# Cross-attention on one core: x in four buffers instead of one, and the last store in two halves

## The chip, the cores and the metric

The kernel runs on one core of a Trainium2 chip. The metric is the device time of one execution in microseconds (us). The core has five engines that run side by side and meet only at semaphores: TensorE (PE) multiplies matrices, VectorE (DVE) and ScalarE (ACT) work element by element, GpSimd (POOL) reduces over partitions and issues the DMAs that add to what lies at their destination, and SyncE (SP) issues most other DMAs. Each engine works through its own instructions in order; so does each engine's list of DMAs to issue: a DMA whose wait has not ended holds up those behind it.

## What is computed

For each of 8 batches, with x1 = x and x2 = the context, both 512 channels by 1024 positions, 32-bit floats:

```python
q = jnp.einsum('bcn,dc->bnd', x1, Wq) + bq
k = jnp.einsum('bcn,dc->bdn', x2, Wk) + bk[:, None]
v = jnp.einsum('bcn,dc->bdn', x2, Wv) + bv[:, None]
attn = jax.nn.softmax(jnp.einsum('bnd,bdm->bnm', q, k), axis=2)
attn_out = jnp.einsum('bcm,bnm->bcn', v, attn)
return attn_out + x1
```

q and k have 64 channels, v and the result 512.

## The kernel before

The batches run one after the other, but overlap: `period` works on the second half of batch `s` (products of the exponentials with the context, then with the value weights) and, between them, on the scores and exponentials of the next batch `n`, the query projection of the one after it, `nn`, and a load for `nnn`. The order of all instructions on every engine is the order in which the code issues them (`tc.manual_schedule()`); the tile framework adds only the semaphore waits.

The large products are not done plainly: they are split into 2 by 2 blocks and computed with seven block products (the names "11" to "22", "S1" to "S4", "T1" to "T4" and the numbers 1 to 7 are those of Strassen's scheme in Winograd's form), many of them split once more in the same way. The sums of blocks that this needs are made on DVE (`left_stream`, `right_stream`, lines 521 to 543), on ACT with a sign, or by accumulating DMAs that POOL issues: `add_t4` (line 360) adds T2 into T4, which ACT filled with the negative of another block; `right_stream(s, 4, ...)` reads T4 on DVE (line 536, name `eI4eT`). The softmax's denominators go over a small chain: POOL reduces (line 290), a DMA reorders one row (292), DVE takes the reciprocal (298), two DMAs spread it (300, 306), and DVE scales with it (874).

**x.** x is read in a form of 128 partitions by 4 tiles (of 128 channels) by 1024 positions. One buffer with the tag "x" holds it, and it is used by turns: `load_x` (line 133) takes the buffer for x1 of a batch, the query projection reads it, `load_x` takes it again for x2 of the same batch, the key projection reads it, and so on. The four tiles are loaded by four DMAs of 512 KB on SP's queue (line 137). Since a buffer is given anew only when all that touched it has ended, the first of the four waits for all matmuls of the projection before; the other three follow it without such a wait.

**Projections.** `project` (line 182; also `keys_parts`, line 405, for batch 1) does eight products, four tiles by two halves of the positions, tile by tile, and accumulates in one bank. The trace counts 16 matmul records for them (L190 or L413). `next_queries` (line 1127) projects the queries and then loads x2; `next_keys` (line 1134) projects the keys and then loads x1 of the batch after.

**Head.** Batch 0 has its own start (`head`, line 1010). x1 comes in the buffer "x", first its left half in four DMAs (line 1031), then its right half in two DMAs of two tiles each (line 1037); x2 comes in another buffer, in eight DMAs between them (line 1034). Behind these in SP's queue stand four tiles `a` of the context in another layout (line 144) and four tiles of the value weights `w` (line 97). DVE sums two of the `a` tiles at line 109 and then subtracts the maximum from the scores (line 315); ACT takes their exponentials, and the first product (line 463) uses them.

**Tail.** In the last batch x1 stays in the buffer "x", and the result is added into it. POOL adds one block (`tmp[6]`) into two tiles with one DMA (line 1454); DVE adds the others (lines 621, 905, 923, 952, 955) and SP stores each piece as it is ready (lines 924, 953). `finish` (line 957) adds the last two pieces (line 961) and stores them (line 962): 256 KB, then 128 KB of 128 partitions by 256 positions.

SP's DMAs of the whole kernel signal on eight semaphores in turn, and a DMA waits until the one before it on the same semaphore, eight places back, has landed.

Of the kernel before, what the change touches and what calls it, by code (L numbers as in the profile page):

```python
# [15 lines left out]
def kernel(  # L16
# [115 lines left out]

    def load_x(s, x):

        s.x = sb.tile([P, CT, N], F32, tag="x", name=f"x_{s.b}_{x.tensor.name}")
        for c in range(CT):
            nc.sync.dma_start(s.x[:, c, :], x[s.b, ts(c, P), :])

    def load_a(s, *ks):
        for k in ks:  # L140
# [41 lines left out]
    def project(s, nm, w_sb, bank=None):  # L182

        if bank:
            ps = ps_a.tile([P, H], F32, tag=bank, name=f"ps_{nm}_{s.b}")
        else:
            ps = ps_s.tile([P, H], F32, tag="s", name=f"ps_{nm}_{s.b}")
        for c in range(CT):
            for h, r in ((0, lo), (1, hi)):
                nc.tensor.matmul(  # L190
                    ps[r, :],
                    w_sb[:, c, :],
                    s.x[:, c, ts(h, H)],
                    start=(c == 0),
                    stop=(c == CT - 1),
                )
        return ps
# [207 lines left out]
    def keys_parts(s):  # L405

        ps = ps_s.tile([P, H], F32, tag="s", name=f"ps_k_{s.b}")
        s.k = sb.tile([P, H], F32, tag="k", name=f"k_{s.b}")

        def add(*tiles):  # L410
            for c in tiles:
                for h, r in ((0, lo), (1, hi)):
                    nc.tensor.matmul(  # L413
                        ps[r, :], wk_sb[:, c, :], s.x[:, c, ts(h, H)], start=(c == 0), stop=(c == CT - 1)
                    )
            if c == CT - 1:
                nc.scalar.activation(s.k, ps, AF.Identity, bias=bk_sb)

        return add
# [169 lines left out]
    def multiply_573(s):  # L589

        s.inner["o7"], s.inner["o3"] = inner_w["o7"], inner_w["o3"]
        a = [ps_a.tile([P, H], F32, tag=f"a{j}", name=f"ps_oa{j}_{s.b}_7") for j in range(2)]
        chain, third = inner_parts(s, "o7")
        d = [ps_s.tile([P, H], F32, tag="s", name=f"ps_od{j}_{s.b}_3") for j in range(2)]
        for j in range(2):
            s.bank["a", j], s.bank["d", j] = a[j], d[j]
        v = sb.tile([P, H], F32, tag="top", name=f"vo73_{s.b}", bufs=2)
        v7, v3, copy = v[:, left], v[:, right], nc.scalar.copy
        u5 = s.tmp[5] = sb.tile([P, 2, H], F32, tag="u5", name=f"uo5_{s.b}")
        a0, a1, d0, d1 = ([x[:, left], x[:, right]] for x in (*a, *d))  # L600
# [16 lines left out]

        def add_v(k, v):
            r, h = int(k[0]) - 1, int(k[1]) - 1
            x = s.x[:, 2 * r + 1, ts(h, H)].rearrange("p (a n) -> p a n", a=2)  # L620
            nc.vector.tensor_tensor(x, x, v.unsqueeze(1).to_broadcast([P, 2, H // 2]), ALU.add)

        for x in ORDER573:
            if x[0] == 5:
                j, k = divmod(x[1], 2)
                ps = s.bank["c", j]
                nc.tensor.matmul(
                    ps,
                    w["S1"][:, k, ts(j, P)],
                    s.y["T1"][:, k, :],  # L630
                    start=False,
                    stop=k == 1,
                    skip_group_check=True,
                )
                if k == 1:
                    copy(u5[:, j, :], ps)
                    for q in ("22", "12"):
                        with_x1(s, q, j)
            elif x[0] == 4:
                part, k = divmod(x[1], 2)  # L640
                if x[1] == 2:
                    s.bank["last"] = last = ps_a.tile([P, H], F32, tag="c0", name="ps_last")
                if x[1] == 0:
                    last_left(s, True)
                    evict_o(s, "12", rows=(0,))
                ps, j, n = ((a[0], 0, slice(0, H)), (last, 1, left), (a[1], 1, right))[part]
                nc.tensor.matmul(
                    ps[:, n],
                    w["22"][:, k, ts(j, P)],
                    s.y["T4"][:, k, n],  # L650
                    start=part == 1 and k == 0,
                    stop=k == 1,
                    skip_group_check=True,
                )
            else:
                i, z = f"o{x[0]}", x[1]
                ps, opens, copies = steps[x]
                inner_product(s, i, z, ps, opens)
# [242 lines left out]
    def with_x1(s, k, j):  # L901

        r, h = int(k[0]) - 1, int(k[1]) - 1
        x = s.x[:, 2 * r + j, ts(h, H)]
        nc.vector.tensor_tensor(x, x, s.tmp[6 if k == "21" else 5][:, j, :], ALU.add)

    def evict_o(s, k, hook=None, rows=range(2)):
# [11 lines left out]

        if s.b == B - 1:  # L920
            for j in rows:
                o = s.x[:, 2 * r + j, ts(h, H)]
# [24 lines left out]

    def last_left(s, second=False):

        o = s.x[:, 3, left]  # L950
        if second:
            nc.vector.tensor_tensor(o, o, s.bank["last"][:, left], ALU.add)
            nc.sync.dma_start(out[s.b, ts(3, P), left], o)
        else:
            nc.vector.scalar_tensor_tensor(o, s.bank["a", 1][:, left], bv_sb[3], o, ALU.add, ALU.add)

    def finish(s):

        for j, n in ((0, slice(0, H)), (1, right)):
            o = s.x[:, 2 + j, n]  # L960
            nc.vector.scalar_tensor_tensor(o, s.bank["a", j][:, n], bv_sb[2 + j], o, ALU.add, ALU.add)
            nc.sync.dma_start(out[s.b, ts(2 + j, P), n], o)

    def add_tile(s, h, i):
        nc.gpsimd.dma_start(s.mx[h], s.e[h][:, :, i, :], accum_op=ALU.add)  # L965
# [11 lines left out]
    def head_queries(s, x_sb, h, n, bank=None):  # L977
# [6 lines left out]
        def add(*tiles):  # L984
            for c in tiles:
                for r in (lo, hi):
                    nc.tensor.matmul(
                        ps[r, n], wq_sb[:, c, :], x_sb[:, c, ts(h, H)][:, n], start=(c == 0), stop=(c == CT - 1)
                    )
            if c == CT - 1:  # L990
                nc.scalar.activation(s.q[:, ts(h, H)][:, n], ps[:, n], AF.Identity, bias=bq_sb)
# [18 lines left out]
    def head(s):  # L1010
# [5 lines left out]

        s.q = sb.tile([P, N], F32, tag="q", name=f"q_{s.b}", bufs=2)
        s.k = sb.tile([P, H], F32, tag="k", name=f"k_{s.b}")
        x1_sb = sb.tile([P, CT, N], F32, tag="x", name="x1_head")
        x2_sb = sb.tile([P, 2, MH, H], F32, tag="e1", name="x2_head")  # L1020
        s.x = x2_sb.rearrange("p t c (h n) -> p c t h n", h=2)

# [17 lines left out]
        load_a(s, "21", "22", "11", "12")  # L1040
        load_values()
        tiles = range(CT)
# [70 lines left out]
    def period(s, n, nn, nnn):  # L1113
# [337 lines left out]
        if n:  # L1451
            add_x1(s, "21")
        else:
            nc.gpsimd.dma_start(s.x[:, 2:4, 0:H], s.tmp[6], accum_op=ALU.add)
        if s.b == 0:
            negate(n, "S3")
            add_11(n, "S3")
# [111 lines left out]
```

## Time and profile before

| | |
|---|---|
| time, three runs | 665.46, 665.56, 666.08 us (median 665.56) |
| the profiled execution: its time | 666.55 us |
| its span, from the first to the last instruction | 664.7 us |
| PE busy | 659.7 us (99%) |
| DVE busy | 615.8 us (93%) |
| ACT busy | 378.6 us (57%) |
| POOL busy | 224.2 us (34%) |
| granted TensorE clock | 1.0 throughout |
| moved by DMA | 135.88 MB, mean 204 GB/s |

Times in the profile's views are from the start of the span. A "line" such as L137 is the line of the kernel before that issued the instruction; of a helper that is called from several places there is one line. "PE" is a matmul, "PEld" its weight load, "SPq" the queue of SP. A row of the timeline gives start, duration, engine, line, operation, what it writes and reads, how many instructions are merged, and in brackets how long the engine was idle before and what ended that. A row of a line's own view gives the shortest, median and longest duration in nanoseconds and the first and last start; the row "DMA to landing" gives the shortest, median and longest time from the issue of a DMA to its completion.

### The profile page before, as it was taken

The numbers are of one execution on the slowest core, as the hardware profiler recorded it, in microseconds if no ns is written. First come the engines' busy times: TensorE is split into PE (matmuls) and PEld (weight loads), VectorE is DVE, ScalarE is ACT, GpSimd is POOL, SyncE is SP. The second block draws the span as 40 slices with busy tenths as digits, with TensorE's granted clock in tenths as the row PEclk, the third lists the DMA queues.
The fourth block names the chain that finished last, engine by engine and source line by source line (L and its number), as shares of the span: only waits on it lengthen the run. The fifth ranks groups of instructions, "written<-read, shape, count | busy, mean of one in ns | idle before, by whom it ended". The sixth has DMA issues, their size and how long they took to land.

```text
span 664.7 us, 7983 instructions
## 1 busy us (share of the span) xinstructions
PE 659.7 (99%) x2626; PEld 433.7 (65%) x2626; DVE 615.8 (93%) x865; ACT 378.6 (57%) x723; POOL 224.2 (34%) x192
## 2 busy tenths in 40 slices
PE   9999999999999999999999999999999999999997
PEld 5435754757658666686666776666865757666865
DVE  0989999999999989999899989999899999999997
ACT  2855467345574674755756647656467455584332
POOL 0125215531245402553124631254214640244300
PEclk9999999999999999999999999999999999999999
DMA  8688576996799869999599995899946996399504
GB/s 326 260 239 270 142 231 143 188 237 215 233 184 224 237 183 284 160 227 243 168 280 185 253 226 163 259 200 235 267 98 169 207 255 194 73 181 240 128 22 150
DMA packets 51545, 135.88 MB, mean 204 GB/s; under 512 B 5680, under 2 KB 6192, under 8 KB 51504
## 3 DMA queue, kind: packets, MB, share of 16 engines
q0 software_dynamic: 24512, 61.94, 50.1%
q1 hardware_dynamic: 26704, 73.15, 30.7%
q8 instruction: 21, 0.34, 0.2%
q10 hardware_dynamic: 288, 0.28, 0.2%
q14 instruction: 20, 0.16, 0.1%
HBM read 87.83 MB, written 16.81 MB: 157 GB/s over the span
## 4 chain that ended last, share of the span: by engine, by line
PE 96%; DMA 3%; SPq 0%; DVE 0%; issue 0%
PE ps_yc L554 9%; PE ps_oc L463 8%; PE ps_ya L554 7%; PE ps_s L235 6%; PE ps_oa L688 6%; PE ps_oa L463 5%; PE ps_ya L463 4%; PE ps_q L190 4%; PE ps_i5chain L554 3%; PE ps_i4b L839 3%; PE ps_k L190 3%; PE ps_i3chain L554 3%; PE ps_i7chain L554 3%; PE ps_oc L839 3%; PE ps_i2chain L554 3%; PE ps_i1chain L554 3%
## 5 line engine op out<-in xcount | busy, mean ns | idle before, releaser
L330 ACT ACTIVATE e<-e 128x1024 f32<-128x1024 f32 x60 | 63.4, 1059 | 29.3 <-DVE e L321 28.3
L321 DVE TENSOR_TENSOR e<-e,top 128x1024 f32<-128x1024 f32 x60 | 72.7, 1219 | 2.1 <-POOL top L271 2.1
L290 POOL PARTITION_ALL_REDUCE den<-sum x16 | 52.8, 3299 | 63.7 <-DVE sum L265 58.8
L271 POOL PARTITION_ALL_REDUCE top<-max x16 | 29.9, 1868 | 98.3 <-DVE max L265 50.0
L965 POOL DMA_DIRECT2D sum<-e x21 | 25.6, 1219 | 103.0 <-ACT sum L970 39.4
L244 ACT COPY e<-ps_s 128x512 f32<-128x512 f32 x90 | 47.8, 620 | 10.1 <-PE ps_s L235 7.6
L235 PE MATMUL ps_s<-q,k 64*128 64x512 f32 (+1 forms) x188 | 46.9, 599 | 0.0
L255 DVE TENSOR_TENSOR max<-max,e 128x1024 f32<-128x1024 f32 x30 | 36.6, 1220 | 0.3
L235 PEld LDWEIGHTS ps_s<-q,k 64*128 64x128 f32 x188 | 17.4, 186 | 19.9 <-issue 17.3
L874 DVE TENSOR_TENSOR y<-y,den 128x1024 f32<-128x1024 f32 x24 | 29.2, 1222 | 0.3
L463 PE MATMUL ps_oa<-yT,w_S 128*128 128x512 f32 x64 | 28.8, 593 | 0.0
L463 PE MATMUL ps_oc<-yT,w 128*128 128x512 f32 x64 | 28.8, 592 | 0.0
L745 ACT COPY ps_yc<-ps_i7chain 128x256 f32<-128x256 f32 x32 | 11.4, 357 | 30.2 <-PE ps_i7chain L554 24.7
L306 POOL DMA_DIRECT2D den<-row x12 | 6.7, 560 | 59.7 <-DMA row<-few 39.0
L521 DVE TENSOR_TENSOR aI<-a,aI 128x256 f32<-128x256 f32 x60 | 25.3, 422 | 0.6
L521 DVE TENSOR_TENSOR aI<-a 128x256 f32<-128x256 f32 x60 | 25.8, 451 | 0.0
L190 PE MATMUL ps_q<-x_in_x_dram,wqk_sb 128*64 128x512 f32 x112 | 25.6, 598 | 0.0
L745 ACT COPY ps_ya<-ps_i5chain 128x256 f32<-128x256 f32 x32 | 11.5, 360 | 24.1 <-PE ps_i5chain L554 20.0
L745 ACT COPY ps_ya<-ps_i1chain 128x256 f32<-128x256 f32 x28 | 10.0, 357 | 24.7 <-PE ps_i1chain L554 21.1
L554 PE MATMUL ps_yc<-e,aI 128*128 128x256 f32 x92 | 23.6, 379 | 0.0
L688 PE MATMUL ps_oa<-yT,w_S 128*128 128x512 f32 x48 | 23.5, 592 | 0.0
L941 POOL DMA_DIRECT2D r<-in_x_dram x14 | 23.3, 1662 | 0.0
(348 smaller groups left out, 1840.0 us busy)
## 6 DMA issues: line engine op xcount, KB each, us to landing
x_in_x_dram<-in_x_dram SPq DMA_DIRECT2D x60, 512.0 KB, 8.2
a<-in_x2T_dram SPq DMA_DIRECT2D x32, 512.0 KB, 7.1
aS<-in_x2T_dram POOLq DMA_DIRECT2D x21, 512.0 KB, 11.0
sum<-e POOLq DMA_DIRECT2D x21, 512.0 KB, 5.4
eT<-eT POOLq DMA_DIRECT2D x16, 512.0 KB, 11.7
uo<-in_x_dram POOLq DMA_DIRECT2D x14, 512.0 KB, 10.4
r<-in_x_dram POOLq DMA_DIRECT2D x14, 512.0 KB, 8.8
out_dram<-r SPq DMA_DIRECT2D x14, 512.0 KB, 8.4
```

What stands on the lines that cost most here:

```text
L190: nc.tensor.matmul(ps[r, :], w_sb[:, c, :], s.x[:, c, ts(h, H)], start=(c == 0), stop=(c == CT - 1),)
L235: nc.tensor.matmul(ps[g][:, n], s.k[r, ts(i, P)], s.q[r, ts(h, H)][:, n], start=True, stop=True)
L244: nc.scalar.copy(e[:, g, i, :], ps[g])
L255: nc.vector.tensor_tensor(f, e[:, :, 0, :] if i == 1 else f, e[:, :, i, :], op)
L290: nc.gpsimd.partition_all_reduce(s.den[h], s.mx[h][:, 0, :], P, ReduceOp.add)
L321: nc.vector.tensor_tensor(e, e, top, ALU.subtract)
L330: nc.scalar.activation(e, e, AF.Exp)
L463: nc.tensor.matmul(ps, left[ka][:, k, ts(j, P)], right[kb][:, k, :], start=opens and k == 0, stop=i in (2, 3, 4) and k == n_k - 1, skip_gr ...
L521: nc.vector.tensor_tensor(v[k], v[x], v[y], op)
L554: nc.tensor.matmul(ps, s.inner[i][ka][:, k, :], s.inner[i, "t"][kb][:, k, :], start=opens and k == 0, stop=z in (2, 3, 4) and k == n_k - 1 ...
L688: nc.tensor.matmul(ps, w[ka][:, k, ts(j, P)], s.y[kb][:, k, :], start=False, stop=i == 3 and k == 1, skip_group_check=True,)
L839: nc.tensor.matmul(ps, s.inner[i][ka][:, k, :], s.inner[i, "t"][kb][:, k, :], start=opens and k == 0, stop=z in (2, 3, 4) and k == n_k - 1 ...
```

## The change

The buffer of 4 tiles becomes four buffers "x0" to "x3", each of which is given anew when all that read that tile has ended. So each load waits for the matmuls of its own tile. `s.x` becomes a list, and what indexes it follows. The transfers that went over two tiles are split: in the head the two DMAs of the right half of x1 become four, one per tile, and in the tail POOL's one DMA into two tiles becomes two. Besides, the very last store becomes two, partitions 0 to 63 on SP's queue and 64 to 127 on ACT's.

```diff
     def load_x(s, x):
 
-        s.x = sb.tile([P, CT, N], F32, tag="x", name=f"x_{s.b}_{x.tensor.name}")
+        s.x = []
         for c in range(CT):
-            nc.sync.dma_start(s.x[:, c, :], x[s.b, ts(c, P), :])
+            s.x.append(sb.tile([P, N], F32, tag=f"x{c}", name=f"x{c}_{s.b}_{x.tensor.name}"))
+            nc.sync.dma_start(s.x[c], x[s.b, ts(c, P), :])
...
-                    s.x[:, c, ts(h, H)],
+                    s.x[c][:, ts(h, H)],
...
     def finish(s):
 
         for j, n in ((0, slice(0, H)), (1, right)):
-            o = s.x[:, 2 + j, n]
+            o = s.x[2 + j][:, n]
             nc.vector.scalar_tensor_tensor(o, s.bank["a", j][:, n], bv_sb[2 + j], o, ALU.add, ALU.add)
-            nc.sync.dma_start(out[s.b, ts(2 + j, P), n], o)
+            if j:
+                for queue, r in ((nc.sync, lo), (nc.scalar, hi)):
+                    queue.dma_start(out[s.b, ts(2 + j, P), n][r], o[r])
+            else:
+                nc.sync.dma_start(out[s.b, ts(2 + j, P), n], o)
...
-        x1_sb = sb.tile([P, CT, N], F32, tag="x", name="x1_head")
+        x1_sb = [sb.tile([P, N], F32, tag=f"x{c}", name=f"x{c}_head") for c in range(CT)]
...
         for c in range(CT):
-            nc.sync.dma_start(x1_sb[:, c, 0:H], x1[s.b, ts(c, P), 0:H])
+            nc.sync.dma_start(x1_sb[c][:, 0:H], x1[s.b, ts(c, P), 0:H])
...
-        for c in (0, 2):
-            nc.sync.dma_start(
-                x1_sb[:, c : c + 2, H:N], x1[s.b, c * P : (c + 2) * P, H:N].rearrange("(t p) n -> p t n", p=P)
-            )
+        for c in range(CT):
+            nc.sync.dma_start(x1_sb[c][:, H:N], x1[s.b, ts(c, P), H:N])
...
-            nc.gpsimd.dma_start(s.x[:, 2:4, 0:H], s.tmp[6], accum_op=ALU.add)
+            for j in range(2):
+                nc.gpsimd.dma_start(s.x[2 + j][:, 0:H], s.tmp[6][:, j, :], accum_op=ALU.add)
```

More of the change, by code (lines that the diff above doesn't have):

```diff
@@ L413, in add @@
                     nc.tensor.matmul(
-                        ps[r, :], wk_sb[:, c, :], s.x[:, c, ts(h, H)], start=(c == 0), stop=(c == CT - 1)
+                        ps[r, :], wk_sb[:, c, :], s.x[c][:, ts(h, H)], start=(c == 0), stop=(c == CT - 1)
                     )
@@ L619, in add_v @@
             r, h = int(k[0]) - 1, int(k[1]) - 1
-            x = s.x[:, 2 * r + 1, ts(h, H)].rearrange("p (a n) -> p a n", a=2)
+            x = s.x[2 * r + 1][:, ts(h, H)].rearrange("p (a n) -> p a n", a=2)
             nc.vector.tensor_tensor(x, x, v.unsqueeze(1).to_broadcast([P, 2, H // 2]), ALU.add)
@@ L903, in with_x1 @@
         r, h = int(k[0]) - 1, int(k[1]) - 1
-        x = s.x[:, 2 * r + j, ts(h, H)]
+        x = s.x[2 * r + j][:, ts(h, H)]
         nc.vector.tensor_tensor(x, x, s.tmp[6 if k == "21" else 5][:, j, :], ALU.add)
@@ L921, in evict_o @@
             for j in rows:
-                o = s.x[:, 2 * r + j, ts(h, H)]
+                o = s.x[2 * r + j][:, ts(h, H)]
                 nc.vector.scalar_tensor_tensor(o, s.bank[bank, j], bias(j), o, ALU.add, ALU.add)
@@ L948, in last_left @@
     def last_left(s, second=False):
-        o = s.x[:, 3, left]
+        o = s.x[3][:, left]
         if second:
@@ L987, in add @@
                     nc.tensor.matmul(
-                        ps[r, n], wq_sb[:, c, :], x_sb[:, c, ts(h, H)][:, n], start=(c == 0), stop=(c == CT - 1)
+                        ps[r, n], wq_sb[:, c, :], x_sb[c][:, ts(h, H)][:, n], start=(c == 0), stop=(c == CT - 1)
                     )
```

## The prediction

> **What bounds the kernel now.** I read the page's busy times and chain first, then busy time by stretch, then the stretches where TensorE (PE) is not full.
>
> ```profile
> span 664.7 us, 7983 instructions
> ...
> PE 659.7 (99%) x2626; PEld 433.7 (65%) x2626; DVE 615.8 (93%) x865; ACT 378.6 (57%) x723; POOL 224.2 (34%) x192
> ...
> PE 96%; DMA 3%; SPq 0%; DVE 0%; issue 0%
> ```
>
> PE is busy for 659.7 of 664.7 us, and the chain that ends last is 96% PE. All that waits less can give back is the 5.0 us in which PE stands idle, if "busy" is honest; busy time by stretch says where those 5.0 us lie and lets "busy" be tested.
>
> ```profile
> 0.00:25.43 25.43, 24.05 (x140) 13.20 (x140) 9.10 (x14) 9.95 (x19) 1.97 (x5) 1.00 0.90 337
> ...
> 43.15:47.00 3.85, 3.80 (x17) 0.97 (x16) 3.78 (x6) 1.12 (x2) 0.00 (x0) 1.00 0.98 289
> ...
> 198.56:279.09 80.53, 80.53 (x329) 55.01 (x329) 75.95 (x110) 49.53 (x96) 30.08 (x28) 1.00 0.88 217
> ...
> 648.00:664.70 16.70, 13.17 (x49) 8.79 (x47) 11.94 (x21) 4.09 (x11) 0.00 (x0) 1.00 0.47 150
> ```
>
> The columns are the stretch, its length, busy PE, weight load, DVE, ACT and POOL, granted clock, DMA share and GB/s. A batch in the middle of the run (198.56 to 279.09) has PE busy for all 80.53 us. The idle time is 1.4 us in the head (25.43 - 24.05) and 3.5 us in the tail (16.70 - 13.17): 4.9 of the 5.0. Between them one place is open, where the first key projection (L413) waits for x:
>
> ```profile
> 32.50 3.65 PE L190 MATMUL ps_q<-x_in_x_dram,wqk_sb 128*64 128x512 f32 x16
> 36.08 7.13 PE L463 MATMUL ps_yc<-e,a 128*128 128x512 f32 x16
> 43.15 3.93 PE L413 MATMUL ps_k<-x_in_x_dram,wqk_sb 128*64 128x512 f32 x16
> 47.00 7.13 PE L390 MATMUL ps_ya<-eT,aS 128*128 128x512 f32 x16
> ```
>
> ```profile
> 37.65 8.30 DMA x_in_x_dram<-in_x_dram
> 45.95 0.04 issue
> 45.99 1.08 PE ps_k L413 x4
> ```
>
> The first fence is PE's timeline, the second the chain of waits. An unhindered projection takes 36.08 - 32.50 = 3.58 us from its start to the next work's; this one takes 47.00 - 43.15 = 3.85 us. Its fourth tile of x was issued at 37.65 and landed at 45.95, and PE goes on at 45.99. So 0.27 us of 664.7 is what late x costs PE.
>
> **The change part by part.**
>
> *Own buffers for the four tiles.* Before, the first of four loads waits until the whole projection has read x, and the other three follow it. Now the load of tile c waits for the matmuls of tile c alone. A projection of 3.58 us reads a tile in 0.90, so the loads may be issued 2.7, 1.8 and 0.9 us before its end, and the fourth at it; what stands behind them in SP's queue (the q halves, the a tiles, the stores) moves up too, and nothing in it moves back.
>
> ```profile
> SPq L137 <- DMA x_in_x_dram<-in_x_dram: 66.2, 18, 7.6
> SPq L137 <- PE ps_k L190: 50.0, 5, 16.0
> ...
> DMA to landing us min/median/max: 4.4/6.3/8.3
> ```
>
> The first two rows are SP's own waits, the third closes the view of the four loads issued from 36.2 to 37.6. In the second row SP stands waiting for PE, so the lead is real there. At the open place the fourth load leaves at about 36.2, where the first leaves today, instead of 37.65. Landing 4.4 us later (as the first does now) or 8.3 us later (as the fourth does) it is there at 40.6 or 44.5. PE reaches the fourth tile at 43.15 + 3 x 0.90 = 45.8. Either way the wait goes: -0.27 us, with 0 as the other bound. What follows at 47.00 reads exponential sums made before and is not late. At all other projections PE waits for nothing, so there an earlier load is worth 0.
>
> *The head.* The second half of the first x, two transfers, becomes four of half the size, two more places in SP's queue ahead of the a tiles. In the build each SP transfer waits for the landing of the one eight places before it, so each a tile now leaves two places later.
>
> ```profile
> 9.19 3.38 SPq L144 DMA_DIRECT2D a<-in_x2T_dram  x4
> 12.88 3.56 SPq L97 DMA_DIRECT2D w<-in_wvT_dram  x4
> ...
> 18.92 2.81 PE L987 MATMUL ps_q<-x_head,wqk_sb 128*64 128x256 f32 x24
> ...
> 21.74 1.69 DVE L109 TENSOR_TENSOR aS<-a,a 128x1024 f32<-128x1024 f32 x1
> ```
>
> ```profile
> DMA to landing us min/median/max: 7.6/8.2/10.4
> ```
>
> The second fence closes the view of the four a loads. DVE's L109 at 21.74 needs the first two; in the third and fourth place they leave before 12.57 (9.19 + 3.38) and land by 20.8 at the median of 8.2, by 23.0 at the longest. The first costs nothing; the second holds DVE up by 1.3 us, and behind L109 on DVE wait the exponentials' subtractions, which PE's first product waits for. I take 0: in the head's row above the DMA engines are 90% busy at 337 GB/s, the bytes and their order are the old ones, so the landings stay and only the issues move. The four x pieces take the places of the two halves and of the first a tiles, leave by about 11, land by 19.2 at 8.2 us, and PE reads the last two from 18.92 on, the fourth 0.4 us after the third: 0.
>
> *The tail.* POOL's one accumulate into x becomes two of half the size, and the last store two of 64 partitions, on SP and on ACT.
>
> ```profile
> 645.61 1.24 POOL L1454 DMA_DIRECT2D x_in_x_dram<-uo  x1 [20.76 <-ACT uo L474]
> ...
> 652.13 1.89 DVE L621 TENSOR_TENSOR x_in_x_dram<-x_in_x_dram,vo 128x512 f32<-128x512 f32 x3
> ...
> 660.35 1.35 DVE L961 SCALAR_TENSOR_TENSOR x_in_x_dram<-ps_oa,wqk_sb,x_in_x_dram 128x512 f32<-128x512 f32 x2
> ...
> 661.13 0.93 SPq L962 DMA_DIRECT2D out_dram<-x_in_x_dram  x2
> ```
>
> ```profile
> L1024 ACTq DMA_DIRECT2D wqk_sb<-in_wqk_dram x2: 409/434/458, 0.7 to 1.2; - x2
> ```
>
> ```profile
> out_dram<-x_in_x_dram SPq DMA_DIRECT2D x7, 256.0 KB, 2.0
> ...
> x_in_x_dram<-uo POOLq DMA_DIRECT2D x1, 512.0 KB, 4.9
> wqk_sb<-in_wqk_dram ACTq DMA_DIRECT2D x2, 136.0 KB, 4.4
> ...
> out_dram<-x_in_x_dram SPq DMA_DIRECT2D x2, 128.0 KB, 1.9
> ```
>
> The accumulate lands at 650.5 (645.61 + 4.9). Its first reader is the second of L621, at 652.8. Even if the second half leaves only after a full 1.24 us and takes the whole 4.9, it lands at 651.75: 0. The last store leaves when L961 ends, at 661.7. 256 KB take 2.0 us to land, 128 KB 1.9, so 64 KB should take about 1.85: -0.05. The bounds: -0.1, one more step of that size, and +2.5, if ACT's half takes the 4.4 us of the only ACT transfers in the trace. Those ran in the first microseconds beside everything else, so I take the SP rows of the same place and kind.
>
> The Trainium skill, "DMA: Bandwidth & Descriptors", section "Rules for kernel authors", speaks against this part: two transfers to disjoint partition halves share the same 16 DMA engines whichever queues they come from, and one of 128 partitions should be used. By that rule the term is 0 and the sum 0.05 higher; no run so far shows such a pair.
>
> *Sum.* -0.27 + 0 - 0.05 = -0.32 us. The profiled execution took 666.55 us, 1.85 around its span; it would become 666.23. The median of the three runs is 665.56, so I forecast **665.24**, -0.05%. A measurement of this kernel tells no change from about 0.2%, 1.33 us; this lies inside.
>
> **The rivals.**
>
> *The loads brought forward push POOL's accumulates back (slower).* In each of the four middle batches the four x loads leave beside POOL's two accumulates into T4, which DVE reads soon:
>
> ```profile
> L137 SPq DMA_DIRECT2D x_in_x_dram<-in_x_dram x4: 352/822/1290, 223.9 to 226.2; - x4
> DMA to landing us min/median/max: 6.3/10.2/15.1
> ```
>
> ```profile
> L360 POOL DMA_DIRECT2D eT<-eT x2: 1223/1385/1547, 223.7 to 224.2; - x2
> DMA to landing us min/median/max: 12.2/13.9/15.7
> ```
>
> ```profile
> 241.66 1.22 DVE L536 TENSOR_TENSOR eI4eT<-eT 128x1024 f32<-128x1024 f32 x1
> ...
> 248.05 0.69 DVE L536 TENSOR_TENSOR eIo1i<-y 128x512 f32<-128x512 f32 x1
> ```
>
> ```profile
> 250.54 0.59 PE L839 MATMUL ps_oc<-eIo1i,w_I 128*128 128x256 f32 x2
> ```
>
> The second accumulate lands at 239.9 (224.2 + 15.7), 1.8 us before its reader. DVE, in order, then makes the sum that ends at 248.74, 1.8 us before PE's matmul at 250.54. So T4 may be 3.6 us later before PE loses anything; beyond that PE loses the excess, four times. For it: three x tiles that today leave with or after the accumulates go ahead of them. Against: the last x tile lands at 241.3 today, and with the same bytes arriving no later the whole group should be done by then, 1.4 us after 239.9. It needs DMA engines that move less when the order changes; at 5 us of delay it costs 4 x 1.4 = 5.6 us: **670.8**.
>
> On order the Trainium skill, same page, section "Queues, rings and completion order", says that a DMA engine takes turns between queues packet by packet, so POOL's queue would not wait for all of SP's. The trace agrees: accumulates and loads issued together landed interleaved, after 12.2 to 15.7 and 6.3 to 15.1 us.
>
> *ACT's half of the last store lands late (slower).* At 4.4 us in place of 1.9 the end moves by 2.5: 665.56 - 0.27 + 2.5 = **667.8**. It decides from about 1.6 us of extra landing on. For it: the queue carries nothing after those two transfers. Against: nothing else is in flight at the end.
>
> *The loads don't come forward.* The first of SP's rows above has 18 waits of x loads that end with an earlier transfer, not with PE. If the fourth load at 36.2 to 37.6 is held so, the 0.27 stays: **665.5**, no change.
>
> *More is hidden in "busy".* A gain beyond 1.33 us needs head or tail: of their 4.9 us PE's start and the 3.0 us from L961's end to the span's end remain. If the head's loads landed earlier, and its stalls went whole (1.4 us), I would get 665.24 - 1.4 = **663.8**; the order of the first x transfers, which it waits for, is unchanged.
>
> **How the numbers follow.** Chances: the forecast 0.75; loads not forward 0.11; more in the head 0.04; contention 0.05; ACT's half late 0.05. The first two make "same", 0.86; "faster" 0.04; "slower" 0.10. The range: down to 664.5 (the terms at their bounds, 665.19, and 0.6 for the spread of the three runs, 665.46 to 666.08, rounded outwards), up to 666.3 (no gain, 665.56, with the same 0.6 and a little of the head's 1.3).
>
> **What would show it.** Right: L413 followed by L390 after 3.58 us; SP's x loads leaving 0.9 us apart within the projections, the first 2.7 us before their end; L109 still at about 21.7; PE full in the middle batches; both last halves landed within 1.9 us. Wrong: a landing of T4 more than 3.6 us later with idle PE at the o1 products; ACT's half landing after SP's by a microsecond; L109 late by a microsecond; or x loads that still leave after the projection.

## The result, and the profile after

| | before | changed |
|---|---|---|
| median time, 14 executions each, on the same chip | 665.55 us | 667.16 us |
| lowest to highest | 665.17 to 666.41 | 666.10 to 668.03 |
| ratio, 95% interval | | 1.0019 [1.0011, 1.0026] |
| the profiled execution: time, span | 666.55, 664.7 us | 666.10, 664.3 us |

The forecast was 665.24, with 664.5 to 666.3 as its range. The change makes the kernel 1.6 us slower on the medians and 1.4 on the means (667.08 against 665.68). The profiled executions say the opposite, and each is an extreme of its kernel: before's 666.55 lies above all 14 of before's in the table, the changed kernel's is the fastest of its 14. So the two traces show what happens in an execution, but their difference isn't the effect. In the head alone they are 0.76 us apart: the first key projection starts at 42.39 us instead of 43.15. Over the traces of all the runs below, that start scatters from 42.07 to 43.15 with one buffer and from 41.90 to 42.95 with four, so the change isn't shown to move it. Two more measurements, e5 and e11 below, gave 1.0013 [1.0003, 1.0023] and 1.0017 [1.0009, 1.0026].

The page of the changed kernel, its busy times and its chain of waits:

```profile
span 664.3 us, 8017 instructions
...
PE 658.6 (99%) x2626; PEld 433.3 (65%) x2626; DVE 615.9 (93%) x865; ACT 378.4 (57%) x723; POOL 225.5 (34%) x193
...
PE 98%; DMA 1%; DVE 0%; ACTq 0%; issue 0%
```

Busy time by stretch in the changed kernel, the stretches that answer to those of before (length; busy PE, weight load, DVE, ACT and POOL; granted clock; DMA share; GB/s), and PE's timeline at the first key projection:

```profile
0.00:24.68 24.68, 23.13 (x141) 12.71 (x141) 9.11 (x14) 9.95 (x19) 1.97 (x5) 1.00 0.94 358
42.39:45.97 3.58, 3.58 (x17) 1.05 (x16) 3.51 (x6) 0.84 (x2) 0.00 (x0) 1.00 1.04 319
197.50:278.03 80.53, 80.53 (x330) 55.01 (x329) 75.94 (x109) 49.49 (x96) 30.05 (x28) 1.00 0.90 218
647.63:664.33 16.70, 12.52 (x47) 8.46 (x45) 11.28 (x20) 4.09 (x11) 0.00 (x0) 0.97 0.34 127
```

```profile
31.74 3.65 PE L191 MATMUL ps_q<-x_in_x_dram,wqk_sb 128*64 128x512 f32 x16
35.33 7.13 PE L464 MATMUL ps_yc<-e,a 128*128 128x512 f32 x16
42.39 3.65 PE L414 MATMUL ps_k<-x_in_x_dram,wqk_sb 128*64 128x512 f32 x16
45.97 0.70 PE L391 MATMUL ps_ya<-eT,aS 128*128 128x512 f32 x1
```

Where the prediction looked for a gain it is there: the first key projection takes 45.97 - 42.39 = 3.58 us instead of 3.85, and the batch in the middle takes the same 80.53 us, all of them busy. But in a tail of the same length PE is busy for 12.52 us instead of 13.17: 0.65 us more stand idle at the end. The changed kernel's last stores of 128 KB and less (KB each, us to landing; the last two rows are the halves, where the kernel before has one row of 128 KB with 1.9 us, shown in the prediction), then their issues (start, duration):

```profile
out_dram<-x_in_x_dram SPq DMA_DIRECT2D x1, 128.0 KB, 1.9
out_dram<-x_in_x_dram SPq DMA_DIRECT2D x1, 64.0 KB, 2.0
out_dram<-x_in_x_dram ACTq DMA_DIRECT2D x1, 64.0 KB, 2.3
```

```profile
660.70 0.51 SPq L965 DMA_DIRECT2D out_dram<-x_in_x_dram  x1
660.71 0.56 ACTq L965 DMA_DIRECT2D out_dram<-x_in_x_dram  x1
```

SP's own instructions behind the last store, first in the kernel before and then in the changed one (count; shortest, median and longest ns; first to last start):

```profile
L1565 SPq EVENT_SEMAPHORE  x2: 28/28/28, 663.7 to 663.8; - x2
L1565 SPq DRAIN  x2: 7/7/7, 663.8 to 663.9; - x2
```

```profile
L1569 SPq EVENT_SEMAPHORE  x8: 28/28/28, 663.0 to 663.4; - x8
L1569 SPq DRAIN  x2: 7/7/7, 663.5 to 663.6; - x2
```

Two things are read from these rows. Half of the bytes land later, not earlier: the whole 128 KB took 1.96 us from issue to landing in the trace, SP's half 2.04 and ACT's 2.28, 0.3 more. Issuing a half takes 0.51 and 0.56 us of this, issuing the whole store took 0.33. And the kernel ends with SP looking at the eight semaphores of its DMAs, one after the other, 0.06 us each, before the drain. (ACT's few DMAs take their turn among the same eight.) In the kernel before, the last DMA signals the seventh of them; when it has landed two looks are left. In the changed kernel the two more transfers of the head have moved the turn on by two: the last to land, ACT's half (662.99), signals the first that SP looks at, and all eight looks come after its landing. From the landing to the end of the span this makes 1.35 instead of 0.98 us. From the start of the last matmul to the end of the span, the traces give 4.56 us against 3.87: **0.69 us** of tail.

### The profile page after: what moved, and what is told of

The parts are those of the page before. It is cut to its first block, busy times and chain, and to the rows that moved or that the text cites. A ratio compares the mean times of both kernels' runs of the same rounds, so it can differ in the third digit from the quotient of the medians.

```text
span 664.3 us, 8017 instructions
## 1 busy us (share of the span) xinstructions
PE 658.6 (99%) x2626; PEld 433.3 (65%) x2626; DVE 615.9 (93%) x865; ACT 378.4 (57%) x723; POOL 225.5 (34%) x193
## 4 chain that ended last, share of the span: by engine, by line
PE 98%; DMA 1%; DVE 0%; ACTq 0%; issue 0%
PE ps_yc L555 9%; PE ps_oc L464 8%; PE ps_ya L555 7%; PE ps_s L236 6%; PE ps_oa L689 6%; PE ps_oa L464 5%; PE ps_ya L464 4%; PE ps_q L191 4%; PE ps_i5chain L555 3%; PE ps_i4b L840 3%; PE ps_k L191 3%; PE ps_i3chain L555 3%; PE ps_i7chain L555 3%; PE ps_oc L840 3%; PE ps_i1chain L555 3%; PE ps_i2chain L555 3%
```

## The experiments

Times are medians; a ratio stands to the kernel before on the same chip, with its 95% interval. "From the last matmul" is the time from its start to the end of the span.

**e1 to e4: the parts apart.** e1 is the changed kernel with the last store whole; e2 to e4 keep x in one buffer and take the other parts: e2 the two more transfers in the head, e3 the last store in halves as the change has it, and e4 all splits together (POOL's accumulate in two among them). The lines beginning with # say which run an edit belongs to, and "..." stands for lines left out.

```diff
 # e1, from the changed kernel
-            if j:
-                for queue, r in ((nc.sync, lo), (nc.scalar, hi)):
-                    queue.dma_start(out[s.b, ts(2 + j, P), n][r], o[r])
-            else:
-                nc.sync.dma_start(out[s.b, ts(2 + j, P), n], o)
+            nc.sync.dma_start(out[s.b, ts(2 + j, P), n], o)
...
 # e2, from the kernel before
-        for c in (0, 2):
-            nc.sync.dma_start(
-                x1_sb[:, c : c + 2, H:N], x1[s.b, c * P : (c + 2) * P, H:N].rearrange("(t p) n -> p t n", p=P)
-            )
+        for c in range(CT):
+            nc.sync.dma_start(x1_sb[:, c, H:N], x1[s.b, ts(c, P), H:N])
```

> The change with the last store whole again, on SP alone. Theory T (the tail pays: two slower halves and ACT's queue): the time falls to 665.3 to 666.0, within 0.5 us of the kernel before, and the last store lands about 1.95 us after its issue instead of 2.27. Theory L (the loads brought forward cost PE time in some executions) and theory H (the two more transfers in the head do): the time stays at 666.5 to 667.2, 1 to 1.6 us over the kernel before.

> The kernel before with only the right half of the first x loaded in four DMAs instead of two. Theory H: 666.5 to 667.2, over 1 us slower than before. Theories T and L: 665.5 to 666.0, at most 0.4 us slower; those 0.4 us come from SP's last checks, because the last store's semaphore is now checked first of eight, with seven checks of 0.06 us still to come after it lands.

> The kernel before with only the last store in two halves, on SP and ACT. Theory T: slower by 0.3 to 1.6 us (the halves land 0.3 us later in the profile of the change; if ACT's half is later still without the profiler, the whole 1.6). Theories L and H: slower by 0.3 us at most.

> The kernel before with the three split transfers of the change (four DMAs in the head, two of POOL's and two last stores in the tail) but x in one buffer. Theories T and H: as slow as the change plus the 0.27 us of the open place, 667.0 to 667.5. Theory L: 665.9 to 666.5, 0.4 to 0.9 us slower than before from the tail alone.

| | median (before 666.20) | ratio | from the last matmul | landing to the end |
|---|---|---|---|---|
| e1: changed, store whole | 666.49 | 1.0003 [0.9995, 1.0012] | 4.24 | 1.34 |
| e2: two more in the head | 666.73 | 1.0007 [0.9998, 1.0016] | 4.24 | 1.35 |
| e3: store in halves | 666.72 | 1.0004 [0.9996, 1.0013] | 4.15 | 0.97 |
| e4: all splits, one buffer | 666.78 | 1.0009 [1.0000, 1.0017] | 4.54 | 1.34 |

None gives 1.6 us. The expectations reckon with about 665.6 for the kernel before; on this chip it took 666.20, so it is their distances that count. On the means the four lie 0.38, 0.56, 0.37 and 0.73 us above before, and their tails are longer by 0.37, 0.37, 0.28 and 0.67. The traces tell the two terms of the tail apart: e3 has only the later halves (4.15 - 3.87 = 0.28), e2 only the shifted turn (4.24 - 3.87 = 0.37), e4 both. e2 leaves the tail's code as it was, and two transfers in the first 15 us cost it 0.37 us after the last store. SP's instructions at its end:

```profile
L1563 SPq EVENT_SEMAPHORE  x8: 27/28/28, 664.2 to 664.6; - x8
L1563 SPq DRAIN  x2: 7/7/7, 664.7 to 664.7; - x2
```

Between the first key projection and the last matmul the traces of before, of the changed kernel and of e1 to e4 have 613.79 or 613.80 us, all six.

But two of these traces of one buffer show more than the prediction's 0.27 at the first key projection: it takes 4.15 us in e4 and 5.40 in e2 (47.49 - 42.09). The chain of waits in e2, whose fourth load left at 36.59:

```profile
36.59 9.84 DMA x_in_x_dram<-in_x_dram
46.44 0.04 issue
46.48 1.08 PE ps_k L413 x4
```

**e5 to e8: again, and the turn by itself.** e5 is the changed kernel unchanged. e6 has its four buffers, the last store whole, and two of the head's eight transfers of x2 merged, which makes SP's DMAs one more than before in number. e7 is the kernel before with x in two buffers of two tiles. e8 is the kernel before with the store in halves, both on SP.

```diff
 # e6, from the changed kernel (the store as in e1)
-            for c in range(CT):
+            for c in range(CT if t == 0 else 2):
                 nc.sync.dma_start(x2_sb[:, t, c, :], x2h[t, ts(c, P), :])
+        nc.sync.dma_start(x2_sb[:, 1, 2:4, :], x2h[1, 2 * P : 4 * P, :].rearrange("(t p) n -> p t n", p=P))
...
 # e7, from the kernel before (load_x; the transfers of two tiles stay whole)
...
+            if c % 2 == 0:
+                pairs.append(sb.tile([P, 2, N], F32, tag=f"x{c}", name=f"x{c}_{s.b}_{x.tensor.name}"))
+            s.x.append(pairs[-1][:, c % 2, :])
+            nc.sync.dma_start(s.x[c], x[s.b, ts(c, P), :])
...
 # e8, from the kernel before
...
+                for queue, r in ((nc.sync, lo), (nc.sync, hi)):
+                    queue.dma_start(out[s.b, ts(2 + j, P), n][r], o[r])
```

> The changed kernel once more, unchanged, beside the kernel before on one chip. Theory T (the tail costs a fixed 0.69 us: end 4.56 us after the last matmul instead of 3.87, of which 0.3 from later landing halves and 0.37 from the order in which SP checks the DMA semaphores at the end; the shorter wait at L413 gives 0.1 to 0.4 back): end 4.56 us after the last matmul again, ratio 1.0005 to 1.001, about 666.5 to 666.9 where before is 666.2. Rival U (four buffers cost something else that timed executions show and the profiled one does not): ratio 1.0019 again, +1.3 us, with the same tail in the trace. Rival S (a large part of the measured +1.6 us was scatter between executions): ratio under 1.0005.

> The changed kernel with the last store whole, and two of the head's context loads merged into one of the same bytes, so that the number of SP's DMAs is one more than before and the last-landing DMA signals the semaphore that SP checks last. Theory T: the store lands 1.96 us after its issue, the end comes 3.81 us after the last matmul (0.75 less than in the changed kernel, 0.06 less than before), the time is 0.2 to 0.5 us below before. Rival U: the tail as said, but the time is still 0.6 us or more above before. If the check order does not matter: 4.2 us after the last matmul, as with the whole store alone.

> The kernel before with x in two buffers of two tiles each; head loads, accumulate and last store as before, so the number and order of SP's DMAs are the old ones. Theory T: the end comes 3.87 us after the last matmul, L413 takes 3.6 to 3.9 us, the time is 0 to 0.4 us below before. Rival U, where it lies in loads that leave earlier: 0.5 us or more above before.

> The kernel before with the last store in two halves of 64 partitions, both on SP's queue. If the half size is what lands late: both halves take 2.0 us or more to land, and the second, issued 0.3 us behind the first, ends the kernel 0.4 us later than a whole store would, less 0.06 for the semaphore it signals: 4.2 us after the last matmul. If it is the second queue that makes them late (both issues took 0.51 and 0.56 us instead of 0.33): each lands within 1.9 us, and the end comes 4.0 to 4.1 us after the last matmul. The time: 0.1 to 0.4 us above before.

| | median (before 665.93) | lowest to highest | ratio | from the last matmul |
|---|---|---|---|---|
| e5: changed | 666.72 | 665.63 to 668.26 | 1.0013 [1.0003, 1.0023] | 4.56 |
| e6: changed, whole store, one DMA more | 666.89 | 665.39 to 667.36 | 1.0011 [1.0002, 1.0019] | 3.83 |
| e7: two buffers | 665.68 | 665.12 to 666.39 | 0.9997 [0.9988, 1.0005] | 3.86 |
| e8: halves on SP | 666.43 | 666.08 to 667.83 | 1.0012 [1.0003, 1.0021] | 4.43 |

e5's ratio, 1.0013, lies between what its two theories gave (1.0005 to 1.001, and 1.0019). The tail does what was expected of it: 4.56 again, and 3.83 when the last DMA signals the semaphore looked at last. In e8, on one queue, the halves land 1.95 and 2.03 us after their issues, so the 2.28 goes with ACT's queue. The long issue doesn't: here the two issues, one after the other on SP, took 0.51 and 0.59 us, so it goes with the half store of 64 partitions. The second half left 0.56 us behind the first, and 0.56 more is the cost here, above both figures expected for it. The tail isn't all, though: e6's tail is as short as before's, and its median is 0.96 above. Its trace shows a stall in the middle that no other has. Its chain of waits in that stretch, and PE's timeline there:

```profile
297.59 9.43 DMA out_dram<-r
307.01 0.02 issue
307.03 0.04 ACTq L746
307.07 0.04 issue
307.11 0.04 ACT v L746
307.15 0.23 issue
307.38 0.39 ACT ps_ya L746
307.77 0.04 issue
307.81 1.13 PE ps_i5chain L555 x4
```

```profile
305.83 1.03 PE L555 MATMUL ps_ya<-eT,aS 128*128 128x256 f32 x4
307.81 1.13 PE L555 MATMUL ps_i5chain<-eI5aI,aI 128*128 128x256 f32 x4 [0.96 <-ACT ps_ya L746]
```

The store of `r` (line 942, in the changed kernel 943) leaves at 297.59 and lands after 9.43 us. ACT's copy of the third of product 5 (`v`) goes into the buffer that this store reads, and waits; behind it on ACT stands the copy that PE needs, and PE stands idle for 0.96 us. From the first key projection to the last matmul this trace takes 615.24 us instead of 613.80, and 1.23 of these 1.44 us arise here. That store in the kernel before and in e6:

```profile
L942 SPq DMA_DIRECT2D out_dram<-r x1: 372/372/372, 298.5 to 298.5; - x1
...
DMA to landing us min/median/max: 7.3/7.3/7.3
```

```profile
L943 SPq DMA_DIRECT2D out_dram<-r x1: 372/372/372, 297.6 to 297.6; - x1
...
  ACT v L746: 2.4, 1
...
DMA to landing us min/median/max: 9.4/9.4/9.4
```

In the kernel before the x loads leave at 304.48, 1.4 us before this store lands. In e6 they leave from 300.67 on, beside it. Over the four middle batches this store takes 6.6 to 8.0 us in the traces of one buffer and 7.4 to 9.4 in those of four. ACT's copy starts 0.4 us after the start of the third's last matmul where nothing holds it; 1.10 us after it cost PE nothing (e5), 2.37 the stall of e6.

**e9 to e12: that wait taken away.** e9 gives ACT's copy a buffer of its own in the changed kernel, e10 does it in e6; e11 and e12 repeat the changed kernel and e6 beside them.

```diff
+        elif i == 5 and v_tag == "r":
+            v = sb.tile([P, H // 2], F32, tag="v5", name=f"v{i}_{s.b}")
```

> The changed kernel, where ACT's copy of the third of product 5 goes into a small buffer of its own instead of the one that the store of r leaves from. Theory R: in the middle batches the loads of x that leave 3 us earlier slow the store of r (issue to landing 7.7 to 9.4 us instead of 6.6 to 7.9), ACT's copy waits for it, and where it is over 1.4 us late PE stands idle (0.96 us in one trace). Then the copy starts 0.42 us after the third's last matmul in all batches, no row has ACT waiting for the store of r, and the median is 0.3 to 0.8 us below that of the changed kernel on the same chip, with no cluster above 667.2. If that wait is rare and the cost lies only in the tail: median within 0.2 us of the changed kernel.

> The same small buffer, with the last store whole and the number of SP's DMAs one more than before. Theory R with the fixed tail: end 3.8 us after the last matmul, nothing lost in the middle, first key projection 3.6 us: 0.3 to 0.6 us below before (ratio 0.9991 to 0.9995), and 0.8 to 1.2 us below the version without the small buffer. If something else in four buffers costs time: level with or above before.

> The changed kernel once more, to stand beside the version with the small buffer on the same chip. Theory R: in some batch ACT's copy waits for the store of r (0.6 to 2.4 us after the third's last matmul); two clusters of times, near 666.3 and near 667.5; ratio 1.001 to 1.002. If the cost lies only in the tail: one cluster near 0.4 above before.

> Four buffers, last store whole, one DMA more on SP, without the small buffer: to stand beside the version with it on the same chip. Theory R: two clusters, near 665.5 and 666.9, most of the executions in the upper one; median 0.8 to 1.2 us above the version with the small buffer. If the wait for r is not the cause: both versions within 0.3 us.

| | median (before 665.67) | lowest to highest | ratio |
|---|---|---|---|
| e11: changed | 667.01 | 665.79 to 667.66 | 1.0017 [1.0009, 1.0026] |
| e9: with the small buffer | 666.87 | 665.38 to 667.54 | 1.0011 [1.0002, 1.0020] |
| e12: as e6 | 666.23 | 665.51 to 667.09 | 1.0010 [1.0001, 1.0019] |
| e10: as e6, with the small buffer | 666.13 | 665.07 to 666.95 | 1.0006 [0.9997, 1.0014] |

The small buffer does its work (ACT's copy 0.42 us after the start of the third's last matmul in all middle batches) and is worth 0.1 us on the medians. In all five traces with it the stretch from the first key projection to the last matmul takes 613.61 or 613.62 us, 0.2 less than the usual 613.80. The wait for the store of `r` is real, but of the seven traces with four buffers and without the small one only e6's has the long stall, and the expected 0.3 to 1.2 us were wrong. Seven of e9's eleven executions lie between 666.85 and 667.54 and must have another cause. None of these has a trace; e10's profiled execution, the longest of its run, shows a candidate. PE's timeline at its first key projection:

```profile
42.33 1.94 PE L414 MATMUL ps_k<-x_in_x_dram,wqk_sb 128*64 128x512 f32 x8
44.80 1.08 PE L414 MATMUL ps_k<-x_in_x_dram,wqk_sb 128*64 128x512 f32 x4 [0.54 <-DMA x_in_x_dram<-in_x_dram]
46.43 1.08 PE L414 MATMUL ps_k<-x_in_x_dram,wqk_sb 128*64 128x512 f32 x4 [0.55 <-DMA x_in_x_dram<-in_x_dram]
47.44 1.55 PE L391 MATMUL ps_ya<-eT,aS 128*128 128x512 f32 x3
```

47.44 - 42.33 = 5.11 us instead of 3.58, at the place that four buffers were to mend, and much like e2's 5.40 with one. The fourth load left at 35.38 and landed after 11.0 us. The four loads and the accumulate into `a` that POOL issues (line 180, in the changed kernel 181), in e10:

```profile
L138 SPq DMA_DIRECT2D x_in_x_dram<-in_x_dram x4: 328/328/328, 32.8 to 35.4; - x4
...
DMA to landing us min/median/max: 3.9/9.6/11.0
```

```profile
L181 POOL DMA_DIRECT2D a<-in_x2T_dram x1: 1027/1027/1027, 32.8 to 32.8; - x1
...
DMA to landing us min/median/max: 9.7/9.7/9.7
```

In the kernel before the accumulate leaves at 33.59, 2.6 us ahead of the first load, and lands in 5.4 us. With four buffers the first load leaves within 0.1 us of it, the accumulate takes 7.9 to 9.7, and the second to fourth loads land behind it. PE gets to the fourth tile 12.2 us after the accumulate's issue in either kernel, if nothing holds it. Counted from the same issue, the fourth load lands after 12.4 us at the median in the five traces with one buffer that have the accumulate at its old place (11.3 to 13.9), and after 12.0 in the eight with four (10.8 to 13.6). So the fourth load, which leaves 1.45 us earlier than before (2.61 us after the accumulate instead of 4.06), lands some 0.4 us earlier, and a projection that needs it within half a microsecond of its landing still waits now and then: it takes 3.58 to 5.40 us in the five traces (4.13 on average) and 3.58 to 5.11 in the eight (3.83).

**e13 to e16: that accumulate moved.** e14 is e9 with the accumulate one place later on POOL, behind a reduction that holds it to 39 us; e15 the same with e6's tail (all three edits); e16 moves only the accumulate, in the kernel before. e13 repeats the two buffers.

```diff
-            add_11(s, "S3")
             head_second(s, n)
+            add_11(s, "S3")
```

> x in two buffers of two tiles, everything else as before, once more on another chip. If two buffers are better than one (mean 0.48 us below before in the first run of it): ratio 0.999 to 0.9997 again, no time above 666.6, first key projection 3.6 us. If that was scatter: ratio 0.9998 to 1.0005, with times up to 667.

> The changed kernel with ACT's copy in a small buffer of its own, and POOL's accumulate into a of batch 0 one place later, behind the reduction, so that it leaves at 39 instead of 33, after all four x loads. Theory C (the x loads that leave 2.3 us earlier leave together with this accumulate and share the DMA engines with it, so the fourth lands only some 0.4 us earlier, and now and then 1.4 us too late for the first key projection): the fourth x lands before 43, L413 takes 3.58, the cluster 1.4 us above the others is gone, the median is 0.4 to 0.8 us below the usual distance of the changed kernel: ratio 1.0002 to 1.0008, what is left being the 0.69 of the tail. If the cluster has another cause: ratio 1.001 to 1.0015, upper cluster still there, though the fourth x lands early.

> The same, with the last store whole and one SP DMA more than before (end 3.83 us after the last matmul). Theory C with R and the tail: 0.2 to 0.6 us below before, ratio 0.9991 to 0.9997, one cluster. If the cluster has another cause: level with before or up to 0.4 above.

> The kernel before with the accumulate into a of batch 0 one place later on POOL. Theory C: the fourth x of L413, which leaves at 36.6 to 37.7 behind the accumulate of 33.6, then has the engines almost alone, lands before 44 and L413 takes 3.58; times over 666.4 become rare; 0.1 to 0.4 us below before. If L413 is not where the scatter comes from: level with before, with the same spread.

| | median (before 665.97) | lowest to highest | ratio |
|---|---|---|---|
| e13: two buffers | 665.52 | 665.43 to 665.99 | 0.9992 [0.9984, 1.0001] |
| e14: changed, small buffer, later accumulate | 665.80 | 665.53 to 666.46 | 0.9995 [0.9986, 1.0003] |
| e15: and the short tail | 665.66 | 665.09 to 666.91 | 0.9991 [0.9982, 1.0000] |
| e16: before, later accumulate | 665.96 | 665.48 to 667.72 | 1.0000 [0.9992, 1.0008] |

The four loads in e14:

```profile
L138 SPq DMA_DIRECT2D x_in_x_dram<-in_x_dram x4: 327/328/328, 33.4 to 36.0; - x4
...
DMA to landing us min/median/max: 3.3/5.5/6.9
```

With the accumulate behind them (it leaves at 38.83) the loads land in 6.9 us at most, the fourth 2.6 us before PE needs it, and the executions lie within 0.93 us; e9's, without this edit and on another chip, within 2.16. But e15's, with the same edit, lie within 1.82, and e14's ratio is below the 1.0002 to 1.0008 that were expected. In the kernel before the same edit doesn't change the time (e16): there the accumulate leaves at 38.17, beside loads that left from 35.34 to 36.66, and the fourth still lands only 0.2 us before PE needs it. With two buffers the loads leave at 33.6 to 35.7, a little behind the accumulate instead of with it; in both traces the fourth lands 1.4 us before PE needs it, and e13's executions lie within 0.56, e7's within 1.27.

**e17 and e18: the accumulate alone, and all edits again,** on one chip.

> The changed kernel with POOL's accumulate into a of batch 0 one place later, and nothing else (no small buffer for ACT's copy). Theory C: the fourth x of the first key projection lands before 43, L413 takes 3.58, hardly an execution stands over 667, ratio 1.0002 to 1.0008: the 0.69 of the tail is left, less what the scatter of before adds to its median. If ACT's wait for the store of r, which this kernel keeps, costs much: two clusters 1 us apart and a ratio over 1.001.

> The version with the small buffer, the later accumulate, the whole last store and one SP DMA more, once more on another chip: 0.2 to 0.6 us below before, ratio 0.9991 to 0.9998, and 0.5 to 0.9 us below the version with the later accumulate alone (0.73 of it the tail).

e17 (the changed kernel, the accumulate one place later): 666.41 us, 1.0012 [1.0003, 1.0021], before 665.50; within 1.28 us, and its first key projection takes 3.58. The ratio is above the 1.0002 to 1.0008 expected. Its mean is 0.81 us above before's, and 0.68 of that is its tail. e18 (e15 again): 665.39, 1.0000 [0.9991, 1.0009], 0.89 below e17 on the means, of which tail and ACT's wait were to give 0.73 and more. It isn't below before on this chip, whose executions of before lie close together (665.0 to 666.0 but for one). Its expected 0.2 to 0.6 us didn't come.

No version is shown to be faster than before: two buffers have 0.9997 and 0.9992 in their two measurements, and both intervals reach past 1; all edits together have 0.9991, whose interval ends at 1.0000, and in the repetition 1.0000.

## Why the prediction was wrong

The kernel became slower where a gain of 0.32 us was forecast. The step that is shown to have failed is the tail: its term of -0.05 us measured +0.69. The step "Either way the wait goes: -0.27 us" rested on landing times that didn't hold. What makes up the rest of the loss stays open.

**The bound: right.** PE sets the end, the middle has no idle time, and what can be won or lost lies in the head, at the first key projection and in the tail.

**Own buffers, -0.27: right in where, wrong in how sure.** The loads left as said (32.86, 33.72, 34.58 and 35.44, in a projection of 31.74 to 35.33). The step that failed here is "Landing 4.4 us later ... or 8.3 us later ... it is there at 40.6 or 44.5". It took the durations of one trace, though the fourth load's are 7.2 to 9.8 us over the five traces of one buffer, and it carried them over from a group that left behind POOL's accumulate to one that leaves with it. The landings were 44.57 in the trace shown and 43.5 to 46.4 in the others, 8.2 to 11.0 us after the issue, and PE is at the fourth tile at about 45. So this place takes 0.27 us less than in the trace of before in one execution and 1.3 us more in another (e10). That it is shorter on average (3.83 us against 4.13) agrees with the forecast gain, but thirteen traces that scatter by 1.8 us don't prove it. Moving the accumulate makes the fourth load of four buffers land 6.8 to 7.6 us after its issue in all four traces, 2.0 us or more before PE needs it: that is shown. How often the wait comes isn't, since only the profiled executions have traces.

**"What stands behind them in SP's queue ... moves up too, and nothing in it moves back": wrong for what is in flight.** The store of `r`, ahead of the loads, lands up to 9.4 us after its issue instead of 8.0, and once PE lost 1.2 us by it.

**The head, 0: right in time.** L109 starts at 20.98, not later. But the two transfers more had a price at the other end of the kernel, which this part didn't look for: the turn of the semaphores, 0.37 us.

**The tail, -0.05: the term that was most mis-sized.** It measured +0.69 in the trace shown, and 0.67 to 0.69 in all three traces of the changed kernel. 0.3 of it is the landing: "64 KB should take about 1.85" drew a line through 256 and 128 KB, and halves on two queues took 2.04 and 2.28. The rule of the Trainium skill that the prediction weighed ("DMA: Bandwidth & Descriptors", "Rules for kernel authors": one transfer of 128 partitions rather than two of disjoint halves) pointed the right way: the halves did not help, and the runs add that they cost. The other 0.37 is the order of SP's last looks, for which the prediction had no term.

**The rivals.** The contention on T4 cost nothing. Its two accumulates in the changed kernel, beside x loads that now leave from 220.3 on:

```profile
L361 POOL DMA_DIRECT2D eT<-eT x2: 1226/1388/1550, 222.7 to 223.2; - x2
...
DMA to landing us min/median/max: 12.6/13.9/15.3
```

Here they land as late as before (12.2, 13.9, 15.7). In the other three middle batches the second accumulate takes 15.6, 16.4 and 14.9 us instead of 13.0, 15.4 and 14.6: the direction was right, but the delay stays under the 3.6 us of slack, and PE has no idle time there. Beside the loads of four buffers two other DMAs land later as well, the accumulate into `a` and the store of `r`. "ACT's half of the last store lands late" was right in sign; its 2.5 us were 0.3.

**The account.** Against before on the same chip the changed kernel's mean is 1.39, 0.76 and 1.00 us higher in three measurements. 0.69 is the tail, settled by the traces of e2, e3 and e4. Alone it would have made the first median 666.24, so it doesn't explain the measured 667.16. The rest, 0.1 to 0.7 us, seems to belong to the four buffers and scatters: beyond their longer tails the means lie 0.06 to 0.19 us above before in the four versions of one buffer (e2, e3, e4, e8), but 0.01, 0.49 and 0.55 above in e1, e6 and e12. Late DMAs are a likely cause, and two were seen to stop PE, at the first key projection (e10) and at ACT's copy (e6). But the first of these stops PE with one buffer too (e2), and is no longer on average with four, so it isn't shown to make the difference. On one chip the four versions with the accumulate in its old place (e9 to e12) lie 0.21 to 0.55 above before beyond their tails, and the two with it moved 0.13 above (e17) and 0.03 below (e18). That speaks for the accumulate; but each of these means is uncertain by 0.1 to 0.25 us (the scatter of eleven executions, 0.3 to 0.8, over the root of eleven), so it stays an argument, and how the rest divides is open. And the range was too narrow: it took 0.6 us of spread from three executions, where executions of before alone lay 2.6 us apart on another chip (665.18 to 667.80).

## What to carry to other kernels

Before you bring a load forward, list what is in flight when it will leave, on every queue: here a load that left 1.45 us earlier arrived some 0.4 us earlier, and what was in flight beside it arrived later. A DMA more or less anywhere moves the turn of the completion semaphores; look which of them the last DMA signals, and how many looks the end of the kernel still makes behind it. Where the difference of two traces has the opposite sign from the times, find what spreads from execution to execution, and look for it in several traces of the kernel before as well.

## What was not expected of the hardware

- SP looks at eight DMA semaphores in turn at the end, 0.06 us each; which one the last transfer signals is worth up to 0.4 us (landing to end 0.91, 0.97 and 1.35 us for the eighth, the seventh and the first).
- A store of 64 partitions and 64 KB took longer to issue than one of 128 partitions and 128 KB: 0.51 us on SP and 0.56 on ACT at the same moment, 0.51 and 0.59 one after the other on SP (e8), where the whole took 0.33. The halves landed after 2.04 and 2.28 us (SP, ACT) or 1.95 and 2.03 (both on SP), the whole after 1.96.
- An accumulate of 512 KB that POOL issued landed in 5.4 to 5.8 us when it left 2.6 us ahead of four loads of 512 KB (five traces), and in 7.9 to 9.7 us when it left with the first of them (eight traces).
